# Layer 0 of a graph stack: the fusion softmax moved, zeros in front of the first unit, and the order of VectorE's and SP's work around the scaled transposes

## The chip, the core and the metric

The kernel runs on one core of a Trainium2 chip. Five engines work at the same time, each through its own instructions in order: TensorE (PE, its weight loads PEld), VectorE (DVE), ScalarE (ACT), GpSimd (POOL) and SyncE (SP), which here only issues transfers. The metric is the device time of one execution in microseconds (us), lower is better.

## The reference

128 graphs with 64 nodes of 256 features each go through four layers; after each layer `x = layernorm(x + layer(x, adj))`.

```
layer 0: for five groups g of the first 25 nodes (sizes 25, 9, 7, 6, 6):
    A   = adj[:, idx][:, :, idx] + I;   dinv = deg(A) ** -0.5
    h   = relu(dinv A dinv (x_g  @ W1[g]) + b1[g])      # 256 -> 512
    out = relu(dinv A dinv (h    @ W2[g]) + b2[g])      # 512 -> 256
    fused[:, idx] += softmax(fusion_w)[g] * out
layer 1: (dinv (adj + I) dinv) @ (x @ W) + b
layer 2: a polynomial of degree 3 in adj / rowsum on x @ W.T, then leaky relu
layer 3: five steps of h = GRU(A01.T @ (h @ weight[l]), h);  A01 = (adj != 0)
```

Nodes 25 to 63 get no group in layer 0: for them layer 0 is the layernorm alone ("the others").

## The kernel before

All is float32. **Layer 0** works in 16 *units*. A unit is one group and up to four tiles of whole graphs, so many that the rows of a tile fit 128 partitions (56 graphs of 9 nodes, 64 of 7, 84 of 6, 20 of 25). The groups come in the order 1, 2, 3, 4, 0: units 0 to 2, 3 and 4, 5 and 6, 7 and 8, 9 to 15. For each unit `i`:

- `load0(i)` issues the transfers of the adjacency rows `a` and of the node features `xg`, a pair for each tile and run of consecutive nodes (4 to 16 in all). `a` has three buffers, `xg` six. Units 0 to 2 take `xg` through GpSimd's queue, later ones through SP's.
- `prep(i)` on VectorE: `ae = a + eye0`, the degrees `deg`, `dinv` (the power on GpSimd, `d0r`), `ae * dinv`, then `A0` (rows "A" in the trace), the block matrix, by the mask `block0`. TensorE transposes it into `pT`; VectorE scales that into `AT` (L397), with high priority. These scaled transposes are collected in the list `evictions`.
- `aggregate(i)`: `pa = xg.T @ AT`, copied by ScalarE to `ag`. `hidden(i)`: `ph = W1 @ ag`, relu on ScalarE to `hg`. `support(i)`: `ps = hg.T @ W2`, copied to `s`. `add(i)`: `po = s.T @ AT`, then relu with the softmax weight `gw` and bias `gb2` to `z` on ScalarE, and on VectorE the sum in `F`. For group 0, `finish(i)` transposes back (`pse`), layernorms and stores to the DRAM tensor `xa`.

TensorE's order is written out by hand (`manual_schedule` for PE alone). The loop runs over `i` and issues per stage: `load0(i+3)`, `add(i-1)`, `aggregate(i+1)`, `support(i)`, `prep(i+2)`, `hidden(i+1)`. In time TensorE thus goes `po(i-1)`, `pa(i+1)`, `ps(i)`, `pT(i+2)`, `ph(i+1)`. On the other engines a scheduler chooses the order of the instructions when the kernel is built; `tc.issue_after(ins)` adds an edge, so that what is inside comes after `ins`. At run time each engine takes its instructions strictly in that order, SP and its transfers too, and an instruction that waits holds all behind it. Each transfer also waits until the eighth transfer before it, on one of eight lanes that SP's and ScalarE's issues share, has landed.

The **others** are ten pieces `xo` of 128 x 4 x 256 (512 KB): loaded on SP, a layernorm on VectorE (statistics L133 and L134, a power `rs` on GpSimd, four or three multiplies L153), and stored to the DRAM tensor `xb`. Layer 1 reads `xa` and `xb` back (`load_x`). **Layers 1 and 2** are the generator `mid`, for two chunks woven into units 9 to 14; **layer 3** takes most of the time: the GRU's products in a seven-product scheme (L716), with nothing in it that the change touches.

Two smaller steps matter here. The softmax of `fusion_w` (L607 to L619: `fm`, the exp `fe` on ScalarE, `fs`, `fr`, `gw`, `gb2`) is issued at stage -1, after the first scaled transpose. `brz` (L632), needed in layer 3, adds two biases that GpSimd's queue loads at stage 1. The weights `W1[g]`, `W2[g]` (512 KB each) are loaded on SP: group 1 at the start, groups 2 and 3 by stage 0, and groups 4 and 0 all together at stage 0.

Of the kernel before, what the change touches and what calls it, by code (L numbers as in the profile page):

```python
# [9 lines left out]
F32 = mybir.dt.float32  # L10
# [18 lines left out]
NE = 15  # L29
# [32 lines left out]
NU = len(UNITS)  # L62
XP = 40
EPS_LN = 1e-5


@with_exitstack
def gnn_stack(
# [26 lines left out]
    nc = tc.nc  # L95
# [14 lines left out]

        return const(bass.AP(tensor=src.tensor, offset=src.offset, ap=[[0, 128], [1, n]]), [128, n], name, eng, pool)

    powers, evictions = [], []

    def inv_sqrt(v, n, p, name):

# [38 lines left out]
    def layernorm(y, by="v", n=NP, r=128):  # L155
        norm_apply(y, *norm_stats(y, by, n, r), by, n, r)
# [175 lines left out]
    with ExitStack() as c0:  # L332
# [9 lines left out]
        def load0(i, after=None):  # L342

            u = UNITS[i]

            qa = [nc.scalar, nc.sync] if i == 0 else [nc.sync]
            qx = nc.gpsimd if i < 3 else nc.sync
            a = work.tile([TR, 4, NJ], F32, name="a", bufs=3)
            xg = work.tile([TR, 4, D], F32, name="xg", bufs=6)
            for t, (b0, nb) in enumerate(u.tiles):  # L350
                b = slice(b0, b0 + nb)
                row = 0
                for f, m in RUNS[u.g]:
                    rows = slice(row, row + nb * m)
                    row += nb * m
                    w = u.n if u.g < 2 else NE
                    qa[t % len(qa)].dma_start(a[rows, t, :w], adj[b, f : f + m, 0:w])
                    with tc.issue_after(after.ins) if after else nullcontext():
                        qx.dma_start(xg[rows, t, :], x[b, f : f + m, :])
            loads[i] = a, xg  # L360

        def prep(i):

            u = UNITS[i]
            a, xg = loads.pop(i)
            ae = work.tile([TR, 4, NJ], F32, name="ae", bufs=2)
            A0 = work.tile([TR, 4, TR], F32, name="A0", bufs=1)
            AT = work.tile([TR, 4, TR], F32, name="AT", bufs=4)
            p = psum0("pT").rearrange("p (t n) -> p t n", t=4)
            scale = []  # L370
            for ts, nb, r, k in u.same:
                w, c = ts.stop - ts.start, 0
                for f, m in [(0, u.n)] if u.g < 2 else RUNS[u.g]:
                    nc.vector.tensor_add(
                        ae[:r, ts, c : c + m], a[:r, ts, f : f + m], eye0[:r, k, None, c : c + m].to_broadcast([r, w, m])
                    )
                    c += m
                av = ae[:r, ts, : u.n]
                deg = small.tile([TR, w], F32, name="deg")
                nc.vector.tensor_reduce(deg[:r], av, AX.X, ALU.add)  # L380
                dinv = inv_sqrt(deg[:r], w, r, "d0")
                nc.vector.tensor_mul(av, av, dinv[:, :, None].to_broadcast([r, w, u.n]))
                o, c = 0, 0
                for _, m in RUNS[u.g]:
                    nc.vector.tensor_mul(
                        A0[:r, ts, o : o + nb * m].rearrange("p t (b n) -> p t b n", n=m),
                        ae[:r, ts, None, c : c + m].to_broadcast([r, w, nb, m]),
                        block0[:r, None, k, o : o + nb * m].rearrange("p t (b n) -> p t b n", n=m)
                        .to_broadcast([r, w, nb, m]),
                    )  # L390
                    o, c = o + nb * m, c + m
                for t in range(ts.start, ts.stop):
                    nc.tensor.transpose(p[:r, t, :r], A0[:r, t, :r], ident[:r, :r])
                scale.append((AT[:r, ts, :r], p[:r, ts, :r], dinv[:, :, None].to_broadcast([r, w, r])))
            for v in scale:
                with tc.high_priority():
                    evictions.append(nc.vector.tensor_mul(*v))  # L397
            A[i] = AT, xg
# [16 lines left out]
        def hidden(i):  # L415
            u = UNITS[i]
            ag0 = AG.pop(i)
            hg = keep.tile([128, 4, 512], F32, tag="NI", name="hg", bufs=2)
            for e in range(4):
                p = psum0("ph")[:, : u.cols]  # L420
                for k in range(2):
                    nc.tensor.matmul(  # L422
                        p, W1[:, u.g, k, e * 128 : (e + 1) * 128], ag0[:, k, : u.cols], start=k == 0, stop=k == 1
                    )
                nc.scalar.activation(hg[:, e, : u.cols], p, AF.Relu, bias=b1[:, u.g * 4 + e : u.g * 4 + e + 1])
            HG[i] = hg

        def support(i):
# [84 lines left out]

        def others(i):

            layernorm(XO[i], n=XO[i].shape[1])

        def store_others(i):
            t = XO.pop(i)
            nc.sync.dma_start(xb[:, NP * i : NP * i + t.shape[1], :], t)  # L520

        eye0 = const(c_eye0, [TR, 5, NJ], "eye0", nc.scalar, w0)
        load0(0)
        ident = const(c_ident, [128, 128], "ident", nc.scalar)
        block0 = w0.tile([TR, 5, TR], F32, name="block0")
        for ks in (slice(1, 2), slice(2, 5), slice(0, 1)):
            nc.scalar.dma_start(block0[:, ks], c_block0[:, ks])
        nc.vector.memset(F, 0.0)
        b1 = const(b1T, [128, NG * 4], "b1", nc.scalar, w0)
# [35 lines left out]
        for i in range(-2, NU + 1):  # L565
# [21 lines left out]
            if i == -2:  # L587
                load0(1, powers[0])
                load_second(1)
                load0(2, powers[0])  # L590
                load_first(2)
            elif i == -1:
                load_second(2)
                load_first(3)
            elif i == 0:
                load_second(3)
                for g in (4, 0):
                    load_first(g)
                    load_second(g)
            early_stage(i, 2)  # L600
            for f, j in ((store_others, i - 1), (others, i), (load_others, i + 2)):
                for o in range(10):
                    if min(o + 1, 9) == j:
                        f(o)
            if i == -1:

                with tc.issue_after(evictions[0].ins):  # L607
                    fm = small.tile([128, 1], F32, name="fm")
                    nc.vector.tensor_reduce(fm, fw, AX.X, ALU.max, negate=True)
                    fe = small.tile([128, NG], F32, name="fe")  # L610
                    nc.scalar.activation(fe, fw, AF.Exp, bias=fm)
                    fs = small.tile([128, 1], F32, name="fs")
                    nc.vector.reduce_sum(fs, fe, axis=AX.X)
                    fr = small.tile([128, 1], F32, name="fr")
                    nc.vector.reciprocal(fr, fs)
                    gw = w0.tile([128, NG], F32, name="gw")
                    nc.vector.tensor_scalar(gw, fe, fr, None, op0=ALU.mult)
                    gb2 = w0.tile([128, NG, 2], F32, name="gb2")
                    nc.vector.tensor_mul(gb2, b2c.rearrange("p (g k) -> p g k", k=2), gw[:, :, None].to_broadcast([128, NG, 2]))  # L619
            elif i == 1:  # L620
# [8 lines left out]
                    bhh = const_later(bhhT, [128, 6], "bhh")  # L629
                    mask = const_later(maskT, [128, B // 2], "mask")  # L630
                brz = wp.tile([128, 4], F32, name="brz")
                nc.vector.tensor_add(brz, bih[:, 0:4], bhh[:, 0:4])  # L632
            elif i == 4:

                ih = keep.tile([128, 4, 2, D], F32, tag="RZ", name="ih", bufs=2)
                wl = keep.tile([128, 4, 2, D], F32, tag="RZ", name="wl", bufs=2)
                wls = [wl[:, l] for l in range(4)] + [ih[:, 3]]
                with tc.issue_after(powers[-1].ins):
                    for q in range(3):
                        nc.gpsimd.dma_start(ih[:, q], wihT[:, q * D : (q + 1) * D].rearrange("(k p) e -> p k e", p=128))  # L640
                    for l in range(L):
                        nc.gpsimd.dma_start(wls[l], wlT[l].rearrange("(k p) e -> p k e", p=128))
            elif i == g0:
                for c in (0, 1):
                    load_adj(c)
            elif i == g0 + 1:
                for c in (0, 1):
                    load_x(c)
# [8 lines left out]
    WHH = work.tile([128, 3, 7, 128], F32, name="WHH")  # L657
    V = [work.tile([128, 3, 7, 128], F32, name=f"V{l}") for l in range(L)]

    def factors(w, w21):  # L660

        nc.vector.tensor_add(w[:, 4, :], w21, w[:, 3, :])
        nc.gpsimd.tensor_sub(w[:, 6, :], w[:, 0, :], w21)
        nc.vector.tensor_sub(w[:, 5, :], w[:, 4, :], w[:, 0, :])
        nc.vector.tensor_sub(w[:, 2, :], w[:, 1, :], w[:, 5, :])

    raw21 = []

    def fold():
        w21 = work.tile([128, 3, 128], F32, name="wh21")  # L670
        raw21.append(w21[:, 2, :])
        wv = whhT.rearrange("(k p) (q e) -> k p q e", p=128, q=3)
        nc.gpsimd.dma_start(w21, wv[0, :, :, 128:])
        for k in range(2):
            nc.gpsimd.dma_start(WHH[:, :, k, :], wv[k, :, :, :128])
        nc.gpsimd.dma_start(WHH[:, :, 3, :], wv[1, :, :, 128:])
# [352 lines left out]
```

## Time and profile before

| | us |
|---|---|
| median of 3 runs | 2215.38 |
| lowest and highest run | 2215.13, 2219.1 |
| the profiled execution | 2218.77 |
| its span, first to last instruction | 2216.7 |
| PE busy | 2181.5 (98%) |
| PEld, DVE, ACT, POOL busy | 1913.5, 1374.2, 1003.8, 578.5 |
| layer 0 with layers 1 and 2 of the first two chunks | about 0 to 315 of the span |

The profile is one execution. In its rows L397 is a line of the kernel, `AT<-pT,d0o` means "writes AT from pT and d0o", and what follows in brackets is how long the engine stood idle before the row and what it waited for last. A matmul in float32 shows as two passes, so a product of two has twice its count. Rows of TensorE end later than the next one starts because matmuls are pipelined; from start to start is the time they take.

### The profile page before, as it was taken

Reading aid. Unit: us, or ns where it says so; the run is one execution under the profiler, and the core shown is the slowest. Engines: PE = TensorE matmul, PEld = TensorE weight load, DVE = VectorE, ACT = ScalarE, POOL = GpSimd, SP = SyncE. Lnnn points to the kernel's source line nnn. Section 1 sums busy time; section 2 is a strip of 40 time slices with the busy share of each in tenths; the row PEclk is TensorE's granted clock in tenths of the full one; section 3 lists DMA queues with packets and bytes.
Section 4 is the critical chain, followed back from the end, with each engine's and each line's share of the span. In section 5 each row is a group of like instructions: output and inputs, shape, how many; then the busy total and the mean of one; then the engine's idle time right before and its main releaser. Section 6 shows DMA issues by size and latency. Waiting matters only on the chain.

```text
span 2216.7 us, 30151 instructions
## 1 busy us (share of the span) xinstructions
PE 2181.5 (98%) x11530; PEld 1913.5 (86%) x11530; DVE 1374.2 (62%) x3069; ACT 1003.8 (45%) x1853; POOL 578.5 (26%) x639
## 2 busy tenths in 40 slices
PE   7999999999999999999999999999999999999997
PEld 5677888888898889888889898888898898888886
DVE  4443567666666666666766676657666666566546
ACT  2333334445544444445454454455454544455453
POOL 3210123222222223223222222222222232232221
PEclk9999999999999999999999999999999999999999
DMA  6540210000100000000100010001000000000000
GB/s 188 168 129 19 61 46 3 1 3 1 38 4 3 1 20 22 4 1 1 41 1 3 1 41 1 4 1 41 1 1 1 20 10 1 1 10 10 1 1 20
DMA packets 54172, 51.12 MB, mean 23 GB/s; under 512 B 20878, under 2 KB 49036, under 8 KB 54028
## 3 DMA queue, kind: packets, MB, share of 16 engines
q1 hardware_dynamic: 49524, 43.90, 6.5%
q0 software_dynamic: 1936, 4.83, 0.7%
q8 instruction: 91, 1.49, 0.3%
q10 hardware_dynamic: 2568, 0.47, 0.1%
q14 instruction: 53, 0.43, 0.1%
HBM read 32.40 MB, written 16.78 MB: 22 GB/s over the span
## 4 chain that ended last, share of the span: by engine, by line
PE 91%; DMA 3%; DVE 2%; issue 1%; SPq 1%; POOL 1%; ACT 0%; ACTq 0%; POOLq 0%; DVEq 0%
PE parz L716 25%; PE pdrz L716 12%; PE pan L716 12%; PE pa L209 9%; PE pbrz L716 6%; PE pdn L716 6%; PE pT L757 4%; PE pbn L716 3%; PE ps L436 3%; PE pd L306 2%; PE pd L285 2%; PE ph L422 2%; DMA xo<-in_x_dram 1%; PE pa L407 1%; PE po L458 1%
## 5 line engine op out<-in xcount | busy, mean ns | idle before, releaser
L733 ACT COPY c<-parz 128x512 f32<-128x512 f32 x240 | 140.6, 586 | 323.4 <-PE parz L716 322.8
L716 PE MATMUL parz<-Th,WHH 128*128 128x256 f32 x960 | 285.9, 379 | 0.3 <-ACT c L733 0.3
L716 PE MATMUL parz<-Ta,V 128*128 128x256 f32 x960 | 285.5, 379 | 0.0
L696 POOL TENSOR_TENSOR Th<-hn 128x512 f32<-128x512 f32 x64 | 81.4, 1273 | 774.3 <-DVE hn L818 588.6
L815 ACT ACTIVATE NI<-NI,bih 128x512 f32<-128x512 f32 (+1 forms) x162 | 115.9, 715 | 203.7 <-DVE NI L810 203.5
L733 ACT COPY c<-pan 128x512 f32<-128x512 f32 x237 | 138.9, 586 | 149.2 <-PE pan L716 149.2
L716 PEld LDWEIGHTS parz<-Ta,V 128*128 128x128 f32 x960 | 182.4, 190 | 24.8
L716 PEld LDWEIGHTS parz<-Th,WHH 128*128 128x128 f32 x960 | 176.2, 190 | 21.4 <-ACT c L733 0.7
L787 ACT ACTIVATE RZ<-RZ,brz 128x512 f32<-128x512 f32 x160 | 116.0, 726 | 138.9 <-DVE RZ L745 138.9
L696 POOL TENSOR_TENSOR Ta<-agg 128x512 f32<-128x512 f32 x80 | 101.9, 1274 | 260.8 <-ACT agg L213 260.8
L745 DVE TENSOR_TENSOR RZ<-pdrz,c 128x512 f32<-128x512 f32 x80 | 55.1, 688 | 174.1 <-PE pdrz L716 174.1
L716 PE MATMUL pan<-Ta,V 128*128 128x256 f32 x474 | 141.2, 380 | 0.0
L716 PE MATMUL pan<-Th,WHH 128*128 128x256 f32 x474 | 141.0, 379 | 0.0
L138 POOL TENSOR_TENSOR rs<-ve,mhalf 128x4 f32<-128x4 f32 (+3 forms) x67 | 69.0, 1030 | 253.9 <-DVE ve L136 228.2
L739 DVE TENSOR_TENSOR NI<-pbn,c 128x512 f32<-128x512 f32 x79 | 54.7, 692 | 127.7 <-PE pbn L716 108.7
L209 PEld LDWEIGHTS pa<-A,h 128*128 128x128 f32 x1024 | 124.4, 192 | 3.3
L209 PE MATMUL pa<-A,h 128*128 128x128 f32 x1024 | 124.6, 275 | 0.0
L735 DVE TENSOR_TENSOR NI<-pdn,c 128x512 f32<-128x512 f32 x79 | 54.5, 690 | 112.8 <-ACT c L733 112.8
L816 DVE TENSOR_TENSOR RZ<-hn,NI 128x512 f32<-128x512 f32 (+1 forms) x129 | 87.8, 680 | 49.2 <-ACT NI L815 49.2
L818 DVE TENSOR_TENSOR hn<-RZ,NI 128x512 f32<-128x512 f32 (+1 forms) x161 | 109.8, 682 | 1.8
L817 DVE TENSOR_TENSOR RZ<-RZ 128x512 f32<-128x512 f32 (+1 forms) x161 | 109.5, 680 | 1.8
L436 PE MATMUL ps<-W,hg 128*125 128x256 f32 (+5 forms) x464 | 105.6, 385 | 0.0
(217 smaller groups left out, 5077.8 us busy)
## 6 DMA issues: line engine op xcount, KB each, us to landing
out_dram<-xt SPq DMA_DIRECT2D x32, 256.0 KB
W<-in_w_dram SPq DMA_DIRECT2D x10, 512.0 KB
xt<-xb SPq DMA_DIRECT2D x32, 156.0 KB
xo<-in_x_dram SPq DMA_DIRECT2D x9, 512.0 KB
xb<-xo SPq DMA_DIRECT2D x9, 512.0 KB
xt<-xa SPq DMA_DIRECT2D x32, 100.0 KB
xg<-in_x_dram SPq DMA_DIRECT2D x25, 125.0 KB
xa<-xg SPq DMA_DIRECT2D x25, 125.0 KB
```

The costliest lines, as they stand in the source:

```text
L138: nc.gpsimd.tensor_tensor(rs[:r, :n], ve[:r, :n], mhalf[:r, :n], ALU.pow)
L209: nc.tensor.matmul(p[:, q * 128 : (q + 1) * 128], src[:, q, k * 128 : (k + 1) * 128], m[:, q, :], start=True, stop=True)
L436: nc.tensor.matmul(p[: u.rows[t], t - v, :], hg[:, e, u.off[t] : u.off[t] + u.rows[t]], W2[:, u.g, e, :], start=e == 0, stop=e == 3,)
L696: nc.gpsimd.tensor_sub(t[:, 0:2, :], a[:, :, H:], a[:, 0, :].rearrange("p (s n) -> p s n", s=2))
L716: nc.tensor.matmul(bank[:, g, :], w[:, q, i - 1, :], rhs, start=i in (1, 2, 5) and g == 0 and m == 0, stop=m == len(side) - 1, skip_group_ ...
L733: nc.scalar.copy(c, self.a)
L757: nc.tensor.transpose(p[:, q * 128 : (q + 1) * 128], src(q, k), ident)
L787: nc.scalar.activation(RZ[:, q, 0, :], RZ[:, q, 0, :], AF.Sigmoid, bias=b[0])
L815: nc.scalar.activation(n, n, AF.Tanh, bias=bih[:, 4 + j : 5 + j])
L816: e.tensor_sub(d, self.hT[:, j, f], n)
L817: e.tensor_mul(d, d, z)
L818: e.tensor_add(self.hn[:, j, f], d, n)
```

## The change

- `softmax`: issued at stage 0 instead of -1, after the second scaled transpose; its exp also after the fourth relu of unit 0 (new list `relus`).
- Six matmuls of a zero tile (128 x 512, from a buffer of `hg`) into a PSUM bank stand first on TensorE, and the memset of that tile ahead of F's on VectorE.
- `prep`: `ae` comes after the latest scaled transpose issued so far; the layernorm of the others likewise.
- `load0` issues all `a` of a unit, then all `xg` (before: in turn).
- The part of `block0` for group 1 goes through SP's queue, after unit 0's `a` and ahead of `W1[1]`; before it was on ScalarE's, behind `ident`.
- `W1[4]`, `W2[4]`, `W1[0]`, `W2[0]` are loaded at stages 1, 2, 3, 4, one each.
- `brz` is issued at stage 4, after the fifth scaled transpose.

The order of TensorE's instructions is the old one behind the six. On VectorE the built order changes as follows: the `xo` statistics of a piece stand behind an `AT` instead of ahead of one; each unit's `ae` to `A` stand between two `AT`; layer 1's first `Ab` and its degrees stand ahead of `A` and `AT` of unit 7, where before they stood behind `AT` of unit 7. SP's order has the `xg` of units 9, 10 and 11 ahead of layer 1's adjacency `a64`, and the last stores to `xb` later. ScalarE's has the table load first, with no wait on a transfer, and the exp behind four relus.

```diff
--- before.py
+++ after.py
@@ -62,6 +62,7 @@
 NU = len(UNITS)
 XP = 40
 EPS_LN = 1e-5
+WARM = 6
 
 
 @with_exitstack
@@ -110,7 +111,7 @@
 
         return const(bass.AP(tensor=src.tensor, offset=src.offset, ap=[[0, 128], [1, n]]), [128, n], name, eng, pool)
 
-    powers, evictions = [], []
+    powers, evictions, relus = [], [], []
 
     def inv_sqrt(v, n, p, name):
 
@@ -347,16 +348,18 @@
             qx = nc.gpsimd if i < 3 else nc.sync
             a = work.tile([TR, 4, NJ], F32, name="a", bufs=3)
             xg = work.tile([TR, 4, D], F32, name="xg", bufs=6)
+            w = u.n if u.g < 2 else NE
+            runs = []
             for t, (b0, nb) in enumerate(u.tiles):
-                b = slice(b0, b0 + nb)
                 row = 0
                 for f, m in RUNS[u.g]:
-                    rows = slice(row, row + nb * m)
+                    runs.append((slice(row, row + nb * m), t, slice(b0, b0 + nb), slice(f, f + m)))
                     row += nb * m
-                    w = u.n if u.g < 2 else NE
-                    qa[t % len(qa)].dma_start(a[rows, t, :w], adj[b, f : f + m, 0:w])
-                    with tc.issue_after(after.ins) if after else nullcontext():
-                        qx.dma_start(xg[rows, t, :], x[b, f : f + m, :])
+            for rows, t, b, f in runs:
+                qa[t % len(qa)].dma_start(a[rows, t, :w], adj[b, f, 0:w])
+            with tc.issue_after(after.ins) if after else nullcontext():
+                for rows, t, b, f in runs:
+                    qx.dma_start(xg[rows, t, :], x[b, f, :])
             loads[i] = a, xg
 
         def prep(i):
@@ -367,13 +370,14 @@
             A0 = work.tile([TR, 4, TR], F32, name="A0", bufs=1)
             AT = work.tile([TR, 4, TR], F32, name="AT", bufs=4)
             p = psum0("pT").rearrange("p (t n) -> p t n", t=4)
-            scale = []
+            scale, last = [], evictions[-1] if evictions else None
             for ts, nb, r, k in u.same:
                 w, c = ts.stop - ts.start, 0
                 for f, m in [(0, u.n)] if u.g < 2 else RUNS[u.g]:
-                    nc.vector.tensor_add(
-                        ae[:r, ts, c : c + m], a[:r, ts, f : f + m], eye0[:r, k, None, c : c + m].to_broadcast([r, w, m])
-                    )
+                    with tc.issue_after(last.ins) if last else nullcontext():
+                        nc.vector.tensor_add(
+                            ae[:r, ts, c : c + m], a[:r, ts, f : f + m], eye0[:r, k, None, c : c + m].to_broadcast([r, w, m])
+                        )
                     c += m
                 av = ae[:r, ts, : u.n]
                 deg = small.tile([TR, w], F32, name="deg")
@@ -422,7 +426,9 @@
                     nc.tensor.matmul(
                         p, W1[:, u.g, k, e * 128 : (e + 1) * 128], ag0[:, k, : u.cols], start=k == 0, stop=k == 1
                     )
-                nc.scalar.activation(hg[:, e, : u.cols], p, AF.Relu, bias=b1[:, u.g * 4 + e : u.g * 4 + e + 1])
+                relus.append(
+                    nc.scalar.activation(hg[:, e, : u.cols], p, AF.Relu, bias=b1[:, u.g * 4 + e : u.g * 4 + e + 1])
+                )
             HG[i] = hg
 
         def support(i):
@@ -513,17 +519,25 @@
 
         def others(i):
 
-            layernorm(XO[i], n=XO[i].shape[1])
+            with tc.issue_after(evictions[-1].ins):
+                layernorm(XO[i], n=XO[i].shape[1])
 
         def store_others(i):
             t = XO.pop(i)
             nc.sync.dma_start(xb[:, NP * i : NP * i + t.shape[1], :], t)
 
+
+        zero = keep.tile([128, 4, 512], F32, tag="NI", name="zero", bufs=2)[:, 0, :]
+        nc.vector.memset(zero, 0.0)
+        p = psum0("pw")
+        for _ in range(WARM):
+            nc.tensor.matmul(p, zero[:, :128], zero, start=True, stop=True)
         eye0 = const(c_eye0, [TR, 5, NJ], "eye0", nc.scalar, w0)
         load0(0)
+        block0 = w0.tile([TR, 5, TR], F32, name="block0")
+        nc.sync.dma_start(block0[:, 1:2], c_block0[:, 1:2])
         ident = const(c_ident, [128, 128], "ident", nc.scalar)
-        block0 = w0.tile([TR, 5, TR], F32, name="block0")
-        for ks in (slice(1, 2), slice(2, 5), slice(0, 1)):
+        for ks in (slice(2, 5), slice(0, 1)):
             nc.scalar.dma_start(block0[:, ks], c_block0[:, ks])
         nc.vector.memset(F, 0.0)
         b1 = const(b1T, [128, NG * 4], "b1", nc.scalar, w0)
@@ -594,21 +608,21 @@
                 load_first(3)
             elif i == 0:
                 load_second(3)
-                for g in (4, 0):
-                    load_first(g)
-                    load_second(g)
+            elif i < 5:
+                (load_first, load_second)[(i - 1) % 2]((4, 0)[(i - 1) // 2])
             early_stage(i, 2)
             for f, j in ((store_others, i - 1), (others, i), (load_others, i + 2)):
                 for o in range(10):
                     if min(o + 1, 9) == j:
                         f(o)
-            if i == -1:
-
-                with tc.issue_after(evictions[0].ins):
+            if i == 0:
+
+                with tc.issue_after(evictions[1].ins):
                     fm = small.tile([128, 1], F32, name="fm")
                     nc.vector.tensor_reduce(fm, fw, AX.X, ALU.max, negate=True)
                     fe = small.tile([128, NG], F32, name="fe")
-                    nc.scalar.activation(fe, fw, AF.Exp, bias=fm)
+                    with tc.issue_after(relus[3].ins):
+                        nc.scalar.activation(fe, fw, AF.Exp, bias=fm)
                     fs = small.tile([128, 1], F32, name="fs")
                     nc.vector.reduce_sum(fs, fe, axis=AX.X)
                     fr = small.tile([128, 1], F32, name="fr")
@@ -629,8 +643,9 @@
                     bhh = const_later(bhhT, [128, 6], "bhh")
                     mask = const_later(maskT, [128, B // 2], "mask")
                 brz = wp.tile([128, 4], F32, name="brz")
-                nc.vector.tensor_add(brz, bih[:, 0:4], bhh[:, 0:4])
             elif i == 4:
+                with tc.issue_after(evictions[4].ins):
+                    nc.vector.tensor_add(brz, bih[:, 0:4], bhh[:, 0:4])
 
                 ih = keep.tile([128, 4, 2, D], F32, tag="RZ", name="ih", bufs=2)
                 wl = keep.tile([128, 4, 2, D], F32, tag="RZ", name="wl", bufs=2)
...
```

More of the change, by code (lines that the diff above doesn't have):

```diff
@@ L658, in gnn_stack @@
     V = [work.tile([128, 3, 7, 128], F32, name=f"V{l}") for l in range(L)]
+    raw21 = []
     def factors(w, w21):
@@ L665, in factors @@
         nc.vector.tensor_sub(w[:, 2, :], w[:, 1, :], w[:, 5, :])
-    raw21 = []
     def fold():
         w21 = work.tile([128, 3, 128], F32, name="wh21")
-        raw21.append(w21[:, 2, :])
         wv = whhT.rearrange("(k p) (q e) -> k p q e", p=128, q=3)
         nc.gpsimd.dma_start(w21, wv[0, :, :, 128:])
+        raw21.append(w21[:, 2, :])
         for k in range(2):
```

## The prediction

> **What bounds the kernel now.** I read the page's head first, then what TensorE waited for, then the order of time at the start, then the granted clock around each wait. The first fence has two lines of the page, then TensorE's waits from 0 to 140 us (total us, times, longest).
>
> ```profile
> span 2216.7 us, 30151 instructions
> ...
> PEclk9999999999999999999999999999999999999999
> ...
> PE pT L393 <- DVE A L385: 9.8, 1, 9.8
> PE pa L407 <- DVE AT L397: 7.5, 4, 4.5
> PE ph L422 <- ACT ag L412: 3.2, 1, 3.2
> ```
>
> TensorE is busy 98% of the span, so what it stands still is time of the kernel. From 140 us it waits 2.3 us up to 350 us and 4.6 us after that; the change keeps the order of every TensorE instruction and puts six in front. The gain can only be in layer 0, where the three rows hold 20.5 us. The next lines are the start, in order of time (start, duration, operation, idle before and releaser).
>
> ```profile
> 16.57 1.28 ACT L611 ACT_TABLE_LOAD   x1 [16.57 <-DMA fw<-in_fusion_w_dram]
> 18.07 1.04 ACT L412 COPY ag<-pa 128x504 f32<-128x504 f32 x2
> 18.69 9.22 PE L422 MATMUL ph<-ag,W 128*128 128x504 f32 x16 [3.21 <-ACT ag L412]
> 27.74 0.59 PE L393 MATMUL pT<-ident,A 126*126 126x126 f32 x4
> 35.08 1.95 PE L407 MATMUL pa<-AT,xg 126*128 126x126 f32 x16
> 37.18 7.03 PE L422 MATMUL ph<-ag,W 128*128 128x504 f32 x16
> 44.05 1.95 PE L458 MATMUL po<-AT,s 126*128 126x126 f32 x16
> ```
>
> The ScalarE table load stands in front of the fusion softmax's exp and waits until 16.57 us for `fw`; the two copies `ag` that release unit 0's `ph` are queued behind it, although their `pa` had ended by 15.48 us. Then `ph` of unit 0 takes 27.74 - 18.69 = 9.05 us, that of unit 1 44.05 - 37.18 = 6.87 us, with the same shapes: TensorE began at half speed. The page's clock row prints 9 there, so at the start the durations are the evidence, not the clock. Unit 0's first `pa` also took 3.78 us against the 1.95 us at 35.08. The later waits, and the clock second by second after the first of them:
>
> ```profile
> 73.19 2.74 PE L407 MATMUL pa<-AT,xg 112*128 112x112 f32 x16 [1.48 <-DVE AT L397]
> 75.73 8.07 PE L436 MATMUL ps<-W,hg 128*112 128x256 f32 x32
> 129.95 3.78 PE L407 MATMUL pa<-AT,xg 126*128 126x126 f32 x16 [4.46 <-DVE AT L397]
> ```
>
> ```profile
> 73.00:74.00 1.00, 0.81 (x7) 0.81 (x8) 0.96 (x6) 0.00 (x0) 0.00 (x0) 1.00 0.03 7
> 74.00:75.00 1.00, 1.00 (x9) 1.00 (x8) 0.48 (x3) 0.53 (x1) 0.31 (x1) 0.67 0.41 162
> 75.00:76.00 1.00, 1.00 (x6) 1.00 (x6) 0.54 (x5) 0.03 (x1) 0.39 (x1) 0.50 1.13 360
> 76.00:77.00 1.00, 1.00 (x3) 0.66 (x3) 0.32 (x3) 0.50 (x1) 0.47 (x1) 0.50 0.84 168
> 77.00:78.00 1.00, 1.00 (x4) 0.80 (x3) 0.30 (x2) 0.00 (x0) 1.00 (x3) 0.62 0.90 355
> 78.00:80.00 2.00, 2.00 (x11) 1.62 (x10) 0.75 (x3) 0.00 (x0) 2.00 (x4) 1.00 0.78 215
> ```
>
> The columns are stretch, length, busy us of the five engines, granted clock, DMA share, GB/s. A wait of 1.48 us is followed by a clock of 0.67, 0.50, 0.50 and 0.62, which loses (0.33 + 0.50 + 0.50 + 0.38) = 1.71 us more. The same sum from 130 to 137 us (five seconds at 0.50, two at 0.81) is 2.88 us. The 0.84 us wait at 92.86 us leaves the clock at 1.00. What made TensorE wait stands on VectorE:
>
> ```profile
> 44.52 0.16 DVE L632 TENSOR_TENSOR brz<-bih,bhh 128x4 f32<-128x4 f32 x1 [12.82 <-DMA bhh<-in_bhhT_dram]
> ...
> 71.22 1.38 DVE L153 TENSOR_SCALAR xo<-xo,mv,rs 128x256 f32<-128x256 f32 x4 [1.12 <-POOL rs L138]
> 72.52 0.62 DVE L397 TENSOR_TENSOR AT<-pT,d0o 112x448 f32<-112x448 f32 x1
> ```
>
> The scaled transpose `AT` of unit 4 could run when `pT` was done at 64.4 us; it ran at 72.52 us, behind a layernorm of the untouched nodes (`xo`), which had waited for its transfer and for GpSimd's `rs`. At 129.22 us it is the same, behind two such layernorms. The first row is `brz`, which held VectorE 12.8 us for a GpSimd-queued transfer, today under cover: `pa` of unit 2 follows at 45.83 us without a gap.
>
> **The change part by part.** Terms are against the profiled execution (2218.77 us, span 2216.7 us); it lies 3.4 us above the median of 2215.38 us, from which I subtract the same sum.
>
> *Zeros ahead of unit 0.* One memset more on VectorE: F's takes 3.26 us for 3840 columns, so 512 cost 0.43 us; it starts where F's did (1.65 us) and TensorE can begin at 2.1 us. F then ends at 5.35 us, still ahead of `ae` at 5.84 us: no cost. Six 128x512 products are 12 passes; by 0.84 us a pass for the slow 504 columns and 6.87/16 = 0.43 us for the fast, they take 5.2 us at full and 10.2 us at half speed. In this trace steady work began at 18.69 us and passes became short at 23.3 us, 4.6 us later. So 2.1 + 4.6 = 6.7 us covers 5.4 passes, and the other 6.6 take 2.8 us: the zeros end at 9.5 us (8.9 to 10.6 us for an opening after 3.4 to 6.9 us, one to two of the slow stretches seen above; 12.3 us if it never opens). `pT` of unit 0 needs `A`, today at 9.76 us after waiting 0.89 us for `block0`. Its first part goes to SP's queue ahead of W1, costing that queue one issue (0.6 us), and ScalarE's queue loses one. I take `A` at 8.95 us, so the zeros release `pT` at 9.5 us; if `block0` still lands at 9.0 us, 9.8 us. [...]
>
> *Softmax later.* The table load now has no wait and runs while ScalarE is idle; the exp stands behind the four `relu` of unit 0, the five small VectorE steps (0.14 to 0.23 us each) behind `AT` of unit 1. The exp (0.30 us) runs at about 22 us, where ScalarE has nothing until the `ps` copy at 23 us; its results are first used by `z` of unit 0, at about 37 us. Free; uncovered it would be 0.3 us. So unit 0 at full clock: `pT` to `AT` 0.64, `AT` 0.68, handing over 0.06, `pa` 1.79, `ph` 6.87, together 10.05 us. `ph` ends at 9.5 + 10.05 = 19.55 instead of 27.74 us: **8.2 us** (7.1 to 8.7). W1 must be there at 12.7 us; the `b1` issue, which waits for the lane that W1 had taken, went at 8.27 us.
>
> *VectorE edges.* `ae` of a unit now follows the previous unit's `AT`, and the `xo` layernorm follows it too, so no `xo` transfer stands ahead of an `AT`. The stalls at 73.19, 92.86 and 129.95 us go with their clock: (1.48 + 1.71) + 0.84 + (4.46 + 2.88) = **11.4 us**. What is late next is the chain from `AT` through layernorm and `prep` to the next `pT`. Shortest cover, `pT` of unit 3 to `pT` of unit 4: 63.81 - 54.22 = 9.59 us. Chain: to `AT` 0.64, `AT` 0.59, statistics 1.96, `ae` and `brz` 0.45, `rs` and apply 2.41, power and `d0o` 1.5, `ae` 0.2, F 1.14, `A` 0.69: 9.6 us. A tie; I allow **0.5 us** for it. The other stages have 13 to 17.4 us.
>
> *Adjacency first, weights spread, `brz` later.* The number of SP issues per unit is unchanged; `x` rows come up to 8 issues later (8 x 0.74 = 5.9 us), needed only at `pa`, which is a stage after `pT`. VectorE waited 11.0 us for `a` up to 140 us, five times; the longest two (4.84 and 4.47 us) ended at 63.66 and 89.78 us, and the second stood ahead of the `AT` that made the 0.84 us wait, so it is already counted. Four weights of 512 KB leave the burst at 28.5 us, where SP waited 9.2 us on W; the first is needed by unit 7, after 100 us. Nothing is taken for these by themselves; they keep the 8.2 us from being eaten. `brz` is the clearest: with TensorE 8 us earlier, the old place would hold `AT` of unit 2 until 44.6 us against 38 us. In the new place it is reached at about 50 us; `bhh`, issued near 37 us, took 9.0 us, so 46 us. If that cover failed, the tie above would lose what is over.
>
> Sum: 8.2 + 11.4 - 0.5 = 19.1 us; profiled 2199.7 us, from the median 2196.3 us. I say 2196.5 us.
>
> [...]
>
> **The rivals.**
> *Zeros stay slow* (0.12). The trace never shows zeros, and `pa` for 3.8 us did not raise the speed. The zeros would end at 12.3 us, `pT` 2.5 us late; `ph` would start at 18.6 us and end near 27.4 us. Start gain 0.3 instead of 8.2 us: 2204 us.
> *A new wait at unit 7* (0.13). Layer 1's `Ab` now stands on VectorE ahead of `A` and `AT` of unit 7, and waits for `a64`, queued on SP behind 12 `xg` issues of units 9 to 11 (12 x 0.74 = 8.9 us), some of which wait for `pa` of unit 5. Before, `Ab` waited 2.15 us there. I put the landing near 100 us and `pa` of unit 7 at 113 us, 3 us of room after VectorE's queue. If it fails wholly, 7.3 us return: 2204 us.
> *Slower* (0.05). The edges make VectorE serial from each `AT` to the next `A`. If each of some 12 stages ran over its cover by 1.5 us and lost 1.7 us of clock, that is 38 us: 2234 us. It decides from (19.1 + 4.4)/12 = 2.0 us a stage, that is chains of over 17 us where the rows give 10: waits of 5 us or more for `xo` or `a` every stage. Longest today: 2.6 and 4.8 us.
> *It moves waits, not time* (0.06): new stalls of about 15 us; 2215 us.
>
> **How the numbers follow.** The forecast has 0.64. A measurement here tells 0.2%, 4.4 us, from no change. Faster: 0.64 + 0.12 + 0.13 = 0.89; same 0.06; slower 0.05. The range runs from 2192 us (start at its best, and the 2.1 us wait plus clock at 329 us, which I leave as it is, gone as well) to 2206 us, which takes in both 2204 us cases with the 0.5 us bounds: about 0.85.
>
> **What would show it.** Right: `ph` of unit 0 starting near 12.7 us and lasting 6.9 us; no `pa` waiting for `AT` beyond 0.5 us up to 140 us; clock 1.00 from 10 to 320 us; `pT` of unit 9 near 139 instead of 158.08 us. Wrong: half clock after the zeros, a wait of `pa` of unit 7, `AT` rows released by a transfer, or a later part of the trace that is not the old one shifted.

## The result and the profile after

The changed kernel takes 2218.93 us (median of 6 runs, 2217.62 to 2219.9), the kernel before 2217.42 us in the runs beside it (median of 6): ratio 1.0007, 95% interval [0.9994, 1.002]. No change can be told, where the prediction had 2196.5 us. The profiled execution took 2217.88 us with a span of 2216.0 us.

The first fence is what TensorE waited for from 0 to 140 us (total us, times, longest), in the changed kernel.

```profile
PE pT L397 <- DVE A L389: 12.8, 1, 12.8
PE ph L426 <- ACT ag L416: 2.5, 1, 2.5
PE pw L534 <- DVE zero L531: 1.5, 1, 1.5
PE pa L411 <- DVE AT L401: 0.8, 1, 0.8
```

The waits for `AT`, 7.5 us before, have shrunk to the 0.8 us of unit 0, as forecast. But one new wait of 12.8 us stands on top, with a second of 2.5 us behind it. TensorE in order of time (start, duration, operation, idle before and releaser):

```profile
1.49 7.95 PE L534 MATMUL pw<-zero 128*128 128x512 f32 x12 [1.49 <-DVE zero L531]
9.29 0.60 PE L397 MATMUL pT<-ident,A 126*126 126x126 f32 x4
10.65 2.05 PE L411 MATMUL pa<-AT,xg 126*128 126x126 f32 x16 [0.77 <-DVE AT L401]
12.65 7.03 PE L426 MATMUL ph<-ag,W 128*128 128x504 f32 x16
19.51 0.60 PE L397 MATMUL pT<-ident,A 126*126 126x126 f32 x4
...
72.19 0.60 PE L397 MATMUL pT<-ident,A 126*126 126x126 f32 x4
...
89.12 0.48 PE L397 MATMUL pT<-ident,A 126*126 126x126 f32 x3
...
120.00 1.10 PE L397 MATMUL pT<-ident,A 126*126 126x126 f32 x4 [12.84 <-DVE A L389]
123.59 6.74 PE L426 MATMUL ph<-ag,W 128*128 128x264 f32 x16 [2.49 <-ACT ag L416]
...
139.12 0.54 PE L397 MATMUL pT<-ident,A 126*126 126x126 f32 x3
```

The same rows of units 6, 7 and 8 in the kernel before:

```profile
101.66 0.48 PE L393 MATMUL pT<-ident,A 126*126 126x126 f32 x3
...
119.54 0.60 PE L393 MATMUL pT<-ident,A 126*126 126x126 f32 x4
...
140.01 0.54 PE L393 MATMUL pT<-ident,A 126*126 126x126 f32 x3
```

The rows of `pT` are the units: unit 1 at 19.51 us (before 27.74), unit 5 at 72.19 (83.64), unit 6 at 89.12 (101.66). At that point the kernel is 12.5 us ahead. Then unit 7 starts at 120.00 us, where the kernel before had 119.54, and unit 8 at 139.12 (140.01). At unit 9 it is still 0.9 us earlier (157.18 instead of 158.08 us), and the two spans differ by 0.7 us. The whole gain goes back between 107 and 139 us. What VectorE and ScalarE did then:

```profile
94.45 0.16 DVE L121 TENSOR_TENSOR d0s<-deg,d0z 126x4 f32<-126x4 f32 x1
117.77 0.69 DVE L226 TENSOR_TENSOR Ab<-a,pair 128x512 f32<-128x512 f32 x1 [23.16 <-DMA a<-in_adj_dram]
...
119.20 0.75 DVE L389 TENSOR_TENSOR A<-ae,block 126x252 f32<-126x252 f32 x2
```

```profile
97.48 0.72 ACT L468 ACTIVATE z<-po,gb,gw 128x448 f32<-128x448 f32 x1 [0.20 <-PE po L464]
121.94 0.72 ACT L248 ACTIVATE poly<-dg,cw 128x512 f32<-128x512 f32 x1 [23.73 <-DVE dg L244]
122.57 0.71 ACT L468 ACTIVATE z<-po,gb,gw 128x448 f32<-128x448 f32 x1
123.18 0.65 ACT L416 COPY ag<-pa 128x264 f32<-128x264 f32 x2
```

`Ab`, a step of layer 1, waits 23.16 us at the head of VectorE's queue for `a64`. `A` of unit 7, which `pT` of unit 7 needs, stands a few rows behind it. ScalarE is held too: `poly` needs `dg`, which follows `Ab`, and behind `poly` stand the `ag` copies that `ph` of unit 6 needs. Two engines stood still for one transfer. Why it came so late is on SP:

```profile
102.93 7.61 SPq L362 DMA_DIRECT2D xg<-in_x_dram  x8
110.58 2.20 SPq L191 DMA_DIRECT2D a<-in_adj_dram  x2
```

```profile
110.58 7.09 DMA a<-in_adj_dram
117.77 0.69 DVE Ab L226
```

The second of these two fences is from the chain of work in order of time (start, us, what). SP is reached by `a64` only at 110.58 us, after an almost unbroken row of 87 issues since 39.1 us (0.82 us each), and the transfer lands 7.09 us later. Why it takes that long is not shown: from 108 to 112 us the DMA engines were busy to 0.34.

### The profile page after: what moved, and what is told of

The parts are those of the page before. It is cut to its first block, busy times and chain, and to the rows that moved or that the text cites. A ratio compares the mean times of both kernels' runs of the same rounds, so it can differ in the third digit from the quotient of the medians.

```text
span 2216.0 us, 30173 instructions
## 1 busy us (share of the span) xinstructions
PE 2183.2 (99%) x11542; PEld 1910.9 (86%) x11542; DVE 1372.0 (62%) x3070; ACT 1004.3 (45%) x1853; POOL 578.6 (26%) x639
## 4 chain that ended last, share of the span: by engine, by line
PE 95%; DVE 2%; issue 1%; SPq 1%; DMA 1%; POOL 0%; ACT 0%; POOLq 0%; ACTq 0%; DVEq 0%
PE parz L731 25%; PE pdrz L731 12%; PE pan L731 12%; PE pa L210 9%; PE pbrz L731 6%; PE pdn L731 6%; PE ps L442 4%; PE ph L426 4%; PE pT L772 4%; PE pbn L731 3%; PE pd L286 2%; PE pd L307 2%; PE pa L411 1%; PE po L464 1%; PE pp L276 1%
```

## The experiments

The theory: the waiting `Ab` alone took the gain, as everything behind it must wait for a landing that SP's queue fixes near 117.8 us. The main rival: SP's queue is the bound of this stretch, so that a gain of TensorE is lost to late transfers whatever VectorE's order is.

**ab_behind_unit8.** In the changed kernel (code shortened, `...` for lines left as they are):

```
 prep:   evictions.append(...)
+        if i == 8: late.append(evictions[-1])
 mid(c): Ab = keep.tile(...)
+        with tc.issue_after(late[0].ins):
             nc.vector.tensor_mul(Ab, a64, pair)
         ...
+        with tc.issue_after(late[0].ins):
             nc.vector.tensor_reduce(rsum, a64, AX.X, ALU.add)
```

> The changed kernel with one edge more: the first steps of layer 1 that read `a64` (`Ab` and its row sum) stand on VectorE behind the scaled transpose `AT` of unit 8, no longer ahead of `A` of unit 7. Theory 1 (one in-order wait took everything): `Ab` waits for `a64`, which lands at 117.8 us, and `A` of unit 7 stands behind it; with `Ab` out of the way pT of unit 7 starts near 107.3 us instead of 120.0, ph of unit 7 takes 3.7 us, pT of unit 9 starts near 139 us instead of 157.2, TensorE has no wait over 0.5 us up to 140 us, and the time is about 2199 us (18 us below the changed kernel). Rival (SP's queue is the bound): SP issues back to back from 40 to 121 us, so when TensorE comes 12 us earlier, `a` or `xg` of units 8 to 10 are not there; new waits of pT or pa for transfers give back 8 us or more, time 2207 to 2217 us.

Measured: 2199.19 us (median of 5), the kernel before beside it 2218.77 us; ratio 0.9916 [0.9903, 0.993]. TensorE's waits up to 140 us and its rows around unit 7:

```profile
PE pw L539 <- DVE zero L536: 1.5, 1, 1.5
PE pa L416 <- DVE AT L404: 0.8, 1, 0.8
PE ph L431 <- ACT ag L421: 0.6, 1, 0.6
```

```profile
107.26 0.60 PE L400 MATMUL pT<-ident,A 126*126 126x126 f32 x4
107.69 3.73 PE L431 MATMUL ph<-ag,W 128*128 128x264 f32 x16
...
113.04 1.95 PE L416 MATMUL pa<-AT,xg 126*128 126x126 f32 x16
...
120.20 0.54 PE L400 MATMUL pT<-ident,A 126*126 126x126 f32 x3
...
138.27 0.60 PE L400 MATMUL pT<-ident,A 125*125 125x125 f32 x4
```

One edge for two instructions brings 19.7 us against the changed kernel's 2218.93 us, which was measured in other runs, and 19.6 us against the kernel before beside it. (The `ph` at 107.69 us is unit 6's, not unit 7's as the expectation calls it.) The rival falls: the transfers of units 8 to 10 were in time. The later wait of 2.67 us of `pa` of unit 9 in this trace is taken up below.

**ab_behind_unit7.** The same with `if i == 7`: a smaller dose of the same wait.

> The same edge, but one unit earlier: `Ab` behind `AT` of unit 7 and ahead of `A` of unit 8. Theory 1: `AT` of unit 7 ends near 108.7 us, `Ab` then holds VectorE about 9 us until `a64` lands at 117.8 us, and `A` of unit 8 follows about 5 us later, near 123 us, where pT of unit 8 is due near 120.5 us. One wait of pT of unit 8 of 2 to 4 us plus 1.7 us of half clock: about 2203 us. Rival (the landing of `a64` follows TensorE's progress through the buffers of `xg`, so that it moves with the earlier units): no wait, 2199 us; or rival (SP's queue is the bound): 2207 us and more.

Measured: 2205.14 us (one run).

```profile
118.14 0.69 DVE L228 TENSOR_TENSOR Ab<-a,pair 128x512 f32<-128x512 f32 x1 [8.46 <-DMA a<-in_adj_dram]
```

```profile
123.64 0.80 PE L400 MATMUL pT<-ident,A 126*126 126x126 f32 x3 [4.26 <-DVE A L392]
```

`Ab` runs at 118.14 us, about as in the changed kernel (117.77). Now unit 8 pays, 4.26 us and a slow `ph` behind it (8.89 us to the next row, 6.86 us for the same product in ab_behind_unit8), somewhat more than the 2 to 4 us and 2203 us expected. That the landing does not follow TensorE is hardly tested by this run alone, as TensorE had come about equally far in both kernels ahead of the wait (`pT` of unit 6 at 88.48 and 89.12 us). A better test is softmax_early, below: its TensorE is 3.7 us later at unit 7 than in ab_behind_unit8 (110.93 against 107.26 us), and SP still reaches `a64` earlier (108.96 against 112.85 us). In seven kernels with the edges of `prep` and `others` (the changed one, ab_behind_unit8, edges_alone, brz_early, both_waits_moved, no_zeros, softmax_early) SP reaches it between 108.96 and 113.36 us, in the kernel before at 130.10 us. So the date is set by SP's queue, but only to within some us.

**edges_alone.** The kernel before with only the two `issue_after` of `prep` and `others`.

> The kernel before with only the VectorE edges (`ae` and the layernorm of the untouched nodes behind the scaled transpose before them). In the compiled order this alone puts `Ab` ahead of `A` of unit 7. Theory 1: the waits at 73.19 and 92.86 us go (4.0 us with their clock), the one at 129.95 us (7.3 us) is replaced by a wait of pT of unit 7 for `A` behind `Ab`; `a64` lands not before 118 us and pT of unit 7 is due near 115.5 us, so a wait of 5 us or more with its clock; time 2210 to 2217 us. Rival (the edges by themselves take nothing back): 11 us faster, 2206 us.

Measured: 2218.59 us (median of 10), slightly above the expected range; ratio 1.0001 [0.9992, 1.001].

```profile
117.84 0.69 DVE L225 TENSOR_TENSOR Ab<-a,pair 128x512 f32<-128x512 f32 x1 [18.20 <-DMA a<-in_adj_dram]
```

```profile
94.15 0.48 PE L394 MATMUL pT<-ident,A 126*126 126x126 f32 x3
120.07 1.10 PE L394 MATMUL pT<-ident,A 126*126 126x126 f32 x4 [7.87 <-DVE A L386]
```

This is the clearest pair. Without the change's start, TensorE arrives 5.0 us later at unit 6 (94.15 against 89.12 us) and waits 5.0 us less (7.87 against 12.84), and unit 7 starts at the same time (120.07 and 120.00 us). Given the spread of the landing, the agreement to 0.1 us is in part chance. The run also shows which edit put `Ab` there: the edges alone move it from behind `A` of unit 8 to ahead of `A` of unit 7. In the kernel before (`A` of unit 8, then `Ab`):

```profile
129.81 0.62 DVE L385 TENSOR_TENSOR A<-ae,block 126x126 f32<-126x126 f32 x4
...
135.13 0.69 DVE L225 TENSOR_TENSOR Ab<-a,pair 128x512 f32<-128x512 f32 x1 [2.15 <-DMA a<-in_adj_dram]
```

**start_alone.** The kernel before with only the zeros, the later softmax and the first part of `block0` on SP's queue.

> The kernel before with only the start of the change: zeros on TensorE, softmax later, first part of `block0` on SP's queue. `Ab` stays where it was, behind `AT` of unit 7. Theory 1 (a gain at the start lasts only until the next wait that does not depend on TensorE): 8.2 us earlier at pT of unit 1; `brz` at its old place holds VectorE for `bhh`, and returns some of it at `AT` of unit 2 (old landing 44.5 us against a need near 38 us, up to 6 us); the later waits for `xo` transfers, whose landings are set by SP's queue, grow by what is left. 2212 to 2217 us. Rival (the gains of the parts simply add): 2209 us.

Measured: 2215.86 us (median of 10); ratio 0.999 [0.9981, 0.9999].

```profile
43.37 0.16 DVE L642 TENSOR_TENSOR brz<-bih,bhh 128x4 f32<-128x4 f32 x1 [12.82 <-DMA bhh<-in_bhhT_dram]
```

```profile
43.79 2.59 PE L408 MATMUL pa<-AT,xg 126*128 126x126 f32 x8 [5.45 <-DVE AT L398]
```

`pT` of unit 1 is 7.7 us earlier (20.06 us), but `brz` still ends its wait at 43.37 us (44.52 before), so `pa` of unit 2 waits 5.45 us, and half clock follows (0.50 from 41 to 49 us): `pT` of unit 4 is at 65.19 us, later than before the change (63.81). Neither half of the change gains more than 0.2%.

**no_edges.** From here on the base is both_waits_moved, below, for this run and the two after it. Here its two `issue_after` of `prep` and `others` are taken out.

> both_waits_moved without the VectorE edges of the change (`ae` and the layernorm of the untouched nodes may again stand ahead of a scaled transpose). Theory 1 (the edges were worth the waits they removed): layernorms that wait for `xo` again stand ahead of `AT`; pa waits for `AT` at several units of layer 0, together 6 to 12 us with their clock, time 2205 to 2211 us. Rival (with the adjacency first and the weights spread, the transfers come early enough and the edges are no longer needed): no wait of pa over 0.8 us, 2199 us.

Measured: 2212.54 us (one run); `PE pa` waits 9.1 us for `AT` in four places up to 200 us, the longest 3.3 us. That is somewhat above the expected range. Against the 2198.71 us of both_waits_moved, measured in other runs, the edges are worth 13.8 us once `Ab` is out of the way.

**weights_in_burst** and **pairs_in_turn.**

```
-    elif i < 5: (load_first, load_second)[(i - 1) % 2]((4, 0)[(i - 1) // 2])
+    (at i == 0:) for g in (4, 0): load_first(g); load_second(g)
```

> both_waits_moved with the weights of the last two groups loaded in one burst again, as in the kernel before. The prediction took nothing for this edit by itself but held that it protects the gain of the start: theory 1, SP waits for W near 30 us, as in the kernel before (9.2 us), and `a` of units 3 and 4 comes so late that pT of unit 3 or 4 waits 2 to 8 us, 2201 to 2208 us. Rival (cover is wide enough, or the burst costs only SP's own time): no wait over 0.8 us, 2199 us.

```
     for rows, t, b, f in runs:
         qa[t % len(qa)].dma_start(a[rows, t, :w], adj[b, f, 0:w])
-    with ...:
-        for rows, t, b, f in runs:
-            qx.dma_start(xg[rows, t, :], x[b, f, :])
+        with ...:
+            qx.dma_start(xg[rows, t, :], x[b, f, :])
```

> both_waits_moved with the transfers of `a` and `xg` issued in turn again. The prediction took nothing for this edit by itself: theory 1, no wait over 0.8 us of pT or pa up to 160 us, 2199 us. Rival (`a` of a unit is complete up to 5.9 us later, and `A` of units 5 to 8 stands on it): one or more waits of pT for `A` of 1 to 5 us, 2201 to 2206 us.

Measured: 2197.88 and 2198.34 us (one run each), with no wait of TensorE over 0.8 us after the zeros up to 200 us. SP did wait 8.6 us for W in the burst, but TensorE did not feel it: the first theory of weights_in_burst falls, that of pairs_in_turn holds. Neither edit is shown to be worth anything here.

**brz_early.** In ab_behind_unit8, `brz` at its old place in the program, without its `issue_after`.

> ab_behind_unit8 with the sum of biases `brz` at its old place in the program. The prediction held that it would keep `AT` of unit 2 until 44.6 us against a need near 38 us: rival, a wait of pa of unit 2 of about 6 us, 2202 us or more. Theory 1: with the VectorE edges `brz` is compiled behind `A` of unit 3, which stands behind `AT` of unit 2, so it waits for `bhh` where only F and `AT` of unit 3 (needed near 47 us) come after it: no wait over 0.5 us, 2199 us. (In start_alone, without the edges, the wait for `brz` did cost pa of unit 2 5.45 us.)

Measured: 2199.07 us (one run), no such wait. The edges carry `brz` behind `A` of unit 3, where it has cover: `pa` of unit 2 starts at 37.76 us and `pa` of unit 3 at 50.29 us, both without a wait; the edit of its own protects against nothing more.

**no_zeros.** ab_behind_unit8 with `WARM = 0`, the six products left out.

> ab_behind_unit8 without the six products of zeros. Theory 1 (the zeros raise the clock): TensorE begins cold at about 8.7 us, pT of unit 0 takes 1.1, its pa 3.8 and its ph 9.0 us, as in the kernel before, and pT of unit 1 starts near 23.7 us instead of 19.76. As the wait of pa of unit 9 ends with the landing of an `a64` at 142.85 us that SP's queue sets, 2.7 of these 3.9 us are under it: pa of unit 9 waits under 0.3 us, and the time is 1.2 us higher, 2200.5 us (profiled span 2201.6). Rival (the clock rises by itself as soon, and softmax alone made the start): pT of unit 1 near 20 us, time 2199 us, pa of unit 9 still waiting 2.7 us. Rival (losses at the start add up with everything later): 2203 us.

Measured: 2202.35 us (one run).

```profile
8.96 1.10 PE L400 MATMUL pT<-ident,A 126*126 126x126 f32 x4 [8.96 <-DVE A L392]
10.84 3.48 PE L416 MATMUL pa<-AT,xg 126*128 126x126 f32 x16 [0.78 <-DVE AT L404]
14.16 7.02 PE L431 MATMUL ph<-ag,W 128*128 128x504 f32 x16
21.01 0.60 PE L400 MATMUL pT<-ident,A 126*126 126x126 f32 x4
```

A miss: `pT` of unit 1 is only 1.25 us later (19.76 us with the zeros), not 3.9. Without zeros `pT` and `pa` of unit 0 are slow, but `ph` already runs at full speed (21.01 - 14.16 = 6.85 us). `pa` of unit 9 waits 1.74 us instead of 2.67, for an `a64` that is there at 143.17 us (142.85 in ab_behind_unit8), and starts only 0.3 us later: most of the 1.25 us is lost under that date. The time lies within the five runs of ab_behind_unit8 (2198.54 to 2202.43 us), so that the zeros are not shown to be worth anything in the whole kernel.

**softmax_early.** ab_behind_unit8 with the softmax and its exp at their old place (`if i == -1`, `evictions[0]`, no `issue_after` on the exp).

> ab_behind_unit8 with the fusion softmax at its old place. Theory 1: the exp waits for `fw` until about 16.5 us, the `ag` copies behind it release ph of unit 0 near 18.3 us, and TensorE, idle for 6 us after pa, is cold again, so that ph takes 8 to 9 us: pT of unit 1 near 27 us instead of 19.76, of which 2.7 us are under the later wait of pa of unit 9: 2204 us. Rival (the zeros keep the clock up through the gap): ph takes 6.9 us, pT of unit 1 near 25.3 us, 2202 us.

Measured: 2202.57 us (one run).

```profile
14.87 8.72 PE L431 MATMUL ph<-ag,W 128*128 128x504 f32 x16 [2.54 <-ACT ag L421]
23.43 0.60 PE L400 MATMUL pT<-ident,A 126*126 126x126 f32 x4
```

The table load starts at 12.76 us, 3.8 us earlier than in the kernel before (16.57), so less is lost than expected. But after the 2.54 us gap `ph` takes 8.72 us again, although the zeros had run: `pT` of unit 1 is 3.7 us later.

**both_waits_moved.** ab_behind_unit8 with a second edge: the steps on `a64` of later chunks go behind `AT` of unit 10.

```
-        with tc.issue_after(late[0].ins):
+        with tc.issue_after(late[c > 1].ins):      # both places; units 8 and 10
```

> ab_behind_unit8 with a second edge of the same kind: the row sum of the third `a64`, which held VectorE for 9.79 us until 142.85 us and made pa of unit 9 wait 2.67 us at 146.88 us, goes behind `AT` of unit 10. Theory 1 (each wait for an `a64` that stands ahead of a scaled transpose costs its excess, and nothing else is late): pa of unit 9 starts at 144.1 us without a wait, everything after it is 2.7 us earlier, 2196.5 us. Rival (`AT` of unit 9 or 10 is then late for another reason, SP's queue or the layernorm): a wait of 1 us or more returns between 144 and 200 us, 2198 to 2200 us.

Measured: 2198.71 us (median of 5); ratio 0.9913 [0.9899, 0.9926] to the kernel before beside it. In its trace `pT` of unit 10 follows at 150.54 us without a wait, but the median is 0.5 us below ab_behind_unit8, not 2.7. The 2.67 us wait belonged to the profiled execution of ab_behind_unit8, which at 2202.43 us was the slowest of its five. In brz_early, with the same edge, the transfer landed 3.1 us earlier and nothing waited. The second edge is not shown to be worth anything in the median.

## Why the prediction was wrong

The sum came close, in part by luck, and the cap on one rival was wrong. Predicted 19.1 us of gain; the change with `Ab` moved measures 2218.77 - 2199.19 = 19.6 us. But the terms were read from one execution. In edges_alone, whose start is the old one, the gap before `ph` of unit 0 was 1.40 us instead of 3.21, that `ph` ran at full speed, and `pT` of unit 1 stood at 24.54 instead of 27.74 us: against it the start would be worth 5.0 us, not 8.2.

The outcome, no change, is the one that the rival *It moves waits, not time* (0.06) names, without saying which wait. Its sum does not fit: 15 us of stalls would leave about 2196.3 + 15 = 2211 us, not 2215. (The steps of the clock that the prediction calls seconds are microseconds.)

*The start* holds to 0.1 us as a total: `pT` of unit 1 at 19.51 us where 19.55 was worked out, zeros ending at 9.29 us (9.5). Its split was wrong: the prediction laid the slow `ph` of the kernel before on a TensorE that began at half speed. no_zeros (`ph` at 6.85 us, with neither zeros nor a gap) and softmax_early (8.72 us after a gap of 2.54 us, behind zeros) put it on the gap of 3.21 us before it. The rival *Zeros stay slow* did not come: the passes of the zeros shorten from 0.85 to 0.43 us near 6.7 us. Its price rested on the same split; in no_zeros, where TensorE does begin slowly, `pT` of unit 1 loses 1.25 us. The move of `block0` did bring `A` of unit 0 forward, to 7.78 us without a wait (before 9.08 us, after 0.89 us of waiting for it), so the alternative of a landing still at 9.0 us does not hold; the end of the zeros at 9.29 us covers this gain. The table load, which was to wait for no transfer, started at 10.72 us, behind an issue on ScalarE's queue that waited for `b`; it was over by 12.0 us, and `ph` did not wait for it.

*The edges* take the three stalls away, and are worth 13.8 us in the repaired kernel (one run), where 11.4 was summed. *The tie* at unit 4 cost nothing: `pT` of unit 4 has no wait. *Adjacency first, weights spread*: nothing, as taken, but the prediction also held that they keep the 8.2 us from being eaten, and without either of them TensorE has no new wait. *`brz`*: its price without cover was right (start_alone, 43.37 us), but the edges already gave it cover.

*The step that failed* is the rival *A new wait at unit 7*. Its mechanism and its instruction were named, but the sum put the wait at nothing (landing near 100 us, `pa` of unit 7 at 113 us), and three points of it were wrong. First, the landing of `a64`: "near 100 us", measured 117.8 us. Only the last 12 issues were priced; SP's queue had 87 ahead of it since 39.1 us at 0.82 us, and 7.09 us of transfer came after. Second, who waits: not `pa` of unit 7 by way of `AT`, but `pT` of unit 7 by way of `A`, which is due 5.8 us earlier (107.26 against 113.04 us in ab_behind_unit8), and `ph` of unit 6 by way of `poly` on ScalarE, which the prediction didn't see. Third, the price: "if it fails wholly, 7.3 us return" took the stall that the new wait replaced as its bound. The wait ends when SP's queue has brought `a64`, wherever TensorE is, so it returns all the lead gathered ahead of it. The account: 12.84 us of idle; then `pT` of unit 7 to `pT` of unit 8 takes 139.12 - 120.00 = 19.12 us instead of 120.20 - 107.26 = 12.94, of which 2.49 is the second gap and 3.01 the slow `ph` (6.74 against 3.73 us; the granted clock is 0.50 from 119 to 129 us). Together 12.84 + 6.18 = 19.0 us, nearly all of the 19.1 us. The first part is the lead over the kernel before at that point (12.5 us at unit 6); the second comes in place of the stall at 129.95 us, which had been counted as removed with 7.3 us.

What stays open is why the order puts `Ab` there: the runs show that the edges do it, not by which rule of the scheduler. Why `a64` takes 7.09 us from issue to landing is open as well.

## What to carry to other kernels

Here a wait on an in-order queue for a transfer whose landing did not move with TensorE acted as a fixed date: the price of meeting it was the lead at that point (12.84 us of idle) and the half clock after it (0.50 from 119 to 129 us), not the size of the stall that stood there before (4.46 us, 7.3 us with its clock). So list, for every edge that frees a place on an engine, what moves into the place, what that waits for, and count the landing from the transfer's position in the issuing queue. And two halves of a change that bring 0.1% and nothing by themselves can bring 0.9% together, with the one edge that was missing.

## What was not expected of the hardware

In these traces the length of a gap does not tell what clock follows. A gap of 1.48 us in the kernel before cost 1.71 us of clock (0.67, 0.50, 0.50 and 0.62 from 74 to 78 us), and one of 2.54 us in softmax_early was followed by 0.56 and 0.50 from 16 us on. In edges_alone one of 1.40 us was followed by a `ph` at full speed (6.86 us). In no_edges one of 3.25 us was followed by a `pa` of 3.75 us (1.94 us for the same size at 58.36 us in the kernel before), while one of 3.13 us cost nothing (stretch, length, busy us of the five engines, granted clock, DMA share, GB/s):

```profile
124.00:125.00 1.00, 0.00 (x0) 0.00 (x0) 0.10 (x1) 0.29 (x1) 0.85 (x1) 1.00 0.36 121
125.00:126.00 1.00, 0.00 (x0) 0.00 (x0) 1.00 (x4) 0.00 (x0) 0.00 (x0) 1.00 0.32 87
126.00:127.00 1.00, 0.39 (x3) 0.40 (x4) 1.00 (x5) 0.00 (x0) 0.00 (x0) 1.00 0.31 67
127.00:128.00 1.00, 1.00 (x11) 1.00 (x11) 0.86 (x6) 0.14 (x1) 0.00 (x0) 1.00 0.27 86
```

What decides it is not shown.
